# Second attention in quarters: the softmax weights of a query block are divided, turned and copied 32 queries at a time

## The chip, the cores and the metric

The kernel runs on one core of a Trainium2 chip. The metric is the device time of one execution in microseconds. A core has five engines with an instruction queue each: TensorE (PE: matmuls, and transposes as matmuls with an identity), VectorE (DVE), ScalarE (ACT), GpSimd (POOL) and SyncE (SP), which here only issues transfers. Each queue is worked off in order, and an instruction waits on semaphores for what others have to deliver. Matmul results land in PSUM, eight banks of 512 float32 columns on 128 partitions; everything else lies in the on-chip memory SBUF. Indirect transfers (gathers) are issued by GpSimd.

## The reference, cut to what matters

The reference is a network of two layers over `x` of 1 x 2048 x 128. Each layer is an attention and a mixture of experts, with residuals and layer norms. The change is in the second layer's attention, which chooses 96 keys per query: the 64 before it and 32 others by an index score.

```
x = x + attn0(norm(x)); x = x + experts0(norm(x))
x = x + attn1(norm(x)); x = x + experts1(norm(x))

def attn1(x):                                   # 8 heads
    c_kv = x @ W_dkv                            # 32 wide
    s_i = relu(einsum('bthd,bsd->bths', q_i, k_i))
    I = einsum('bths,h->bts', s_i, idx_w)       # index scores
    I = where(causal, -inf, where(local, inf, I))
    _, idx = top_k(I, 96)                       # 64 local, 32 chosen
    key_c, value = (c_kv @ W_uk)[idx], (c_kv @ W_uv)[idx]
    key_r = pope((x @ W_kr)[idx])               # rotated by rank
    scores = (q_c . key_c + q_r . key_r) * (64 + 32) ** -0.5
    attn = softmax(scores)                      # over the 96 keys
    return (attn @ value) @ W_out
```

The first attention has 16 heads of 64 over all 2048 keys (a full softmax); `experts0` takes 4 of 16 experts per token, `experts1` fixed ones of 8 and a shared one.

## The kernel before

**Tiling.** The 2048 tokens are 16 blocks n of 128, and four groups g of 512. The first attention works in 32 units, one for a pair of heads and a group (`UNITS`, line 280), in steps of 512 keys; a unit has four steps, and `run` (line 422) writes them out in order. In a step `by_query` (L323) makes scores by query, VectorE takes their maxima (L329), ScalarE sums exponentials (`sums`, L340); five steps behind, `by_key` (L384, L386) makes the scores again with keys on partitions, ScalarE takes exponentials into a tile `e` of 128 x 2 x 512 (L390), and `mean` (L399) multiplies them with the values, a pair of key blocks behind. The pool `a_e` (`self.ep`, line 274) has six such tiles, shared by `e` and by the temporaries `t_q`, `t_k` of `rope` (L302, L303).

**Beside it.** When a group of 512 queries has passed all eight units, its later stages (`follow`: `experts0`, `attention1`, `experts1`) run as a stream beside the next eight units: `advance` takes so much of the generator as its yields, which are costs in microseconds, allow. The last group's stream runs when the first attention is over (`self.alone`). So groups 0 to 2 are in the background and group 3 alone. The tile framework orders each engine's instructions by their place in the program and by when a cost model thinks them ready, and first attention's maxima and exponentials are raised in priority (`URGENT`); only SP's queue keeps the order in which it was written (`manual_schedule`). An instruction that needs a tile waits until a buffer of its tag is released.

**attention1 (line 725).** For a block of 128 queries: `index_scores` (L802 to L821) and `choose` (L835 to L842) search for the 32 keys of each query by repeated maxima on VectorE; the list is turned (L842), and 32 gathers on GpSimd (L853) bring the chosen rows `kv` of 128 x 32 x 64 from a table in device memory. In the background, gathers are issued by `pay`, one or more for every yield; alone, all at once. `queries` (line 866) loads the local rows `cl` by eight transfers of SP (L873) and makes the queries `ql`, `qs` (L877 to L908). `attend` (line 913) rotates the gathered rows (L97 to L104), turns them into `kr` (L932, L933), and makes the weights: in each quarter b, 32 queries with their 8 heads, two groups of 128 rows, TensorE adds a mask and the scores of 80 local and 128 gathered columns (L942, L950, L956) in a bank `pl`; VectorE takes the maxima (L962, L963); ScalarE writes exponentials and their sums (L966). After all four quarters the sums are inverted (L971), the weights divided (alone by ScalarE, eight instructions, L974; in the background by VectorE, one, L976), and turned on TensorE in four banks `pte` of four transposes (L983), each copied by ScalarE into `eT` (L984). Then the weighted sum of values `po` (L991, L998), its copy `lt` (L1005), the projection `pj` (L1012) and the addition to `xr` (L1013).

**Order in attention1.** Alone: search of 12, of 13, search of 14 with attend(12) beside it, of 15 with attend(13) beside it, then queries and attend of 14, and of 15. In PSUM the background has two banks (`x`, line 138), the stage alone cycles through all eight. `kr` and `eT` share one buffer (tag `w8`).

Of the kernel before, what the change touches and what calls it, by code (L numbers as in the profile page):

```python
# [17 lines left out]
P = 128  # L18
# [88 lines left out]
class Program:  # L107
# [161 lines left out]
    def pools(self):  # L269
        tc = self.tc  # L270

        self.first = ExitStack()
        self.qk = self.first.enter_context(tc.tile_pool(name="a_qk", bufs=3))
        self.ep = self.first.enter_context(tc.tile_pool(name="a_e", bufs=6))
        self.am = self.first.enter_context(tc.tile_pool(name="a_sm", bufs=2))
        self.negs, self.tops = {}, {}
        self.qs, self.ms, self.mrows, self.pos = {}, {}, {}, {}
        self.rs, self.outs, self.pts, self.kcs, self.csq = {}, {}, {}, {}, {}
# [446 lines left out]
    def attention1(self, sc, g):  # L725
# [60 lines left out]
        def pay(us):  # L786

            for _ in range(min(len(gathers), max(1, round(us / 1.8)))):
                gathers.pop(0)[1]()
            return us  # L790
# [75 lines left out]
        def queries(n):  # L866

            cl = sm.tile([80, 8, 32], F32, tag="cl", name=f"cl{n}", bufs=4 if self.alone else 2)  # L870
            for i in range(8):
                lo = max(n * P + 16 * i - 64, 0)
                nc.sync.dma_start(cl[:, i, :], table[lo : lo + 80, 0:32])  # L873
            chosen[n] = chosen[n], cl
            pq = self.x(f"pq{n}", [P, NH1, 64])
            q = slice(P * (n % 4), P * (n % 4) + P)
            nc.tensor.matmul(  # L877
                pq.rearrange("p a b -> p (a b)"), cqT[:, q], self.wq1.rearrange("p a b -> p (a b)"),
                start=True, stop=True,
            )  # L880
            qq = [
                sm.tile([P, 1024], F32, tag="w4", name=f"qq{n}_{i}").rearrange("p (h b d) -> p h b d", h=NH1, b=2)
                for i in range(2)
            ]
            mu = sm.tile([P, NH1, 32], F32, tag="mu", name=f"mu{n}", bufs=1)
            for i in range(2):
                nc.scalar.copy(qq[i][:, :, 0, 0:32], pq[:, :, 0:32])
            softplus(nc, sm, mu, pq[:, :, 32:64], self.one, "spq")
            yield pay(3.0)
            m4 = mu.rearrange("p h (a b) -> p h a b", a=2)  # L890
            for i, at in ((0, n), (1, NT + n)):
                q = qq[i][:, :, 0, :]
                rotate(
                    nc, nc.vector, sm, q[:, :, 32:48], q[:, :, 48:64], m4,
                    bcast(cs[:, 0, at, :], 1, NH1), bcast(cs[:, 1, at, :], 1, NH1), "rq", 1,
                )
                nc.scalar.copy(qq[i][:, :, 1, :], q)
                yield pay(1.5)
            qT = []
            for i in range(2):  # L900
                t = sm.tile([P, P, NH1], F32, tag=f"qT{i}", name=f"qT{n}_{i}", bufs=3 if self.alone else 1)
                for h in range(2):
                    pt = self.x(f"ptq{n}_{i}_{h}")
                    for j in range(4):
                        nc.tensor.transpose(
                            pt[:, j, :], qq[i][:, 4 * h + j, :, :].rearrange("p a b -> p (a b)"), ident
                        )
                    nc.scalar.copy(t[:, :, 4 * h : 4 * h + 4], pt.rearrange("p h q -> p q h"))  # L908
                    yield pay(1.0)
                qT.append(t.rearrange("p q h -> p (q h)"))  # L910
            qTs[n] = qT

        def attend(n):
# [14 lines left out]
            for q in range(4):  # L928
# [3 lines left out]
                    nc.tensor.transpose(pt[:, j, :], kv[:, s : s + 2, :].rearrange("p a b -> p (a b)"), ident)  # L932
                nc.scalar.copy(kr[:, 4 * q : 4 * q + 4, :], pt)  # L933
                yield pay(0.8)
            e = sm.tile([P, 8, NK], F32, tag="e1", name=f"e1_{n}", bufs=1)
            mx = sm.tile([P, 8], F32, tag="mx", name=f"mx1_{n}")
            su = sm.tile([P, 8], F32, tag="su", name=f"su1_{n}")
            ri = sm.tile([P, 8], F32, tag="ri", name=f"ri1_{n}")
            for b in range(4):
                rows = slice(64 * (b // 2), 64 * (b // 2) + 64)  # L940
                pl = self.x(f"pl{n}_{b}", [P, 2, NK])
                nc.tensor.matmul(  # L942
                    pl.rearrange("p a b -> p (a b)"), self.identb,
                    self.smask[:, 1 if n == 0 and b < 2 else 0].rearrange("p a b -> p (a b)"),
                    start=True, stop=False,
                )
                for c in range(2):
                    i = 2 * b + c
                    lo = max(n * P + 16 * i - 64, 0)
                    nc.tensor.matmul(  # L950
                        pl[:, c, 0:80], ql[rows, i * P : i * P + P], kT[rows, lo : lo + 80], start=False, stop=False
                    )
                for c in range(2):
                    for j in range(4):
                        gr = 4 * (2 * b + c) + j
                        nc.tensor.matmul(  # L956
                            pl[32 * j : 32 * j + 32, c, 80:NK], qs[rows, 32 * gr : 32 * gr + 32],
                            kr[rows, gr % 16, :], start=False, stop=(c == 1),
                        )
                yield pay(1.0)  # L960
                m2 = mx[:, 2 * b : 2 * b + 2]
                nc.vector.tensor_reduce(m2, pl, axis=AX.X, op=ALU.max)  # L962
                nc.vector.tensor_scalar(m2, m2, -SCALE1, None, ALU.mult)  # L963
                for c in range(2):
                    i = 2 * b + c
                    nc.scalar.activation(  # L966
                        e[:, i, :], pl[:, c, :], AF.Exp, scale=SCALE1, bias=mx[:, i : i + 1],
                        accum_out=su[:, i : i + 1],
                    )
                yield pay(1.5)  # L970
            nc.vector.reciprocal(ri, su)  # L971
            if self.alone:
                for i in range(8):
                    nc.scalar.activation(e[:, i, :], e[:, i, :], AF.Copy, scale=ri[:, i : i + 1])  # L974
            else:
                nc.vector.tensor_tensor(e, e, bcast(ri, 2, NK), ALU.mult)  # L976
            yield pay(2.0)
            eT = sm.tile([P, 16, P], F32, tag="w8", name=f"eT{n}", bufs=1).rearrange("p (k i) q -> p k i q", k=2)
            for k, (lo, hi) in enumerate(((0, 80), (80, NK))):
                for h in range(2):  # L980
                    pt = self.x(f"pte{n}_{k}_{h}")
                    for j in range(4):
                        nc.tensor.transpose(pt[: hi - lo, j, :], e[:, 4 * h + j, lo:hi], ident)  # L983
                    nc.scalar.copy(eT[: hi - lo, k, 4 * h : 4 * h + 4, :], pt[: hi - lo])  # L984
                    yield pay(0.8)

            po = self.x(f"po1_{n}", [P, 2, P])
            for c in range(2):
# [257 lines left out]
```

## Time and profile before

| what | us |
|---|---|
| median of three runs (2803.74 to 2807.57) | 2804.27 |
| the profiled execution | 2803.35 |
| its span in the trace | 2801.6 |
| TensorE busy | 2538.6 |
| ScalarE busy | 1789.8 |
| VectorE busy | 1670.8 |
| GpSimd busy | 671.3 |

The trace is of one execution. A page gives each engine's busy time, then the span in 40 slices (a digit is the busy share in tenths, and PEclk the clock that was granted to TensorE, in tenths of full speed), and groups of instructions by line, `out<-in`, with the number, the busy time, the mean of one, and the idle time of the engine just before them with what ended it. The timeline lists instructions by start and duration in us; a bracket gives the idle time before one and what ended it. An engine's busy time is an average over stages with different limits: in the table of slices TensorE is at nine tenths for most of the span and lower in the last eighth, where group 3 is alone.

### The profile page before, as it was taken

What the parts mean: (1) busy time and instruction counts of PE and PEld (TensorE: products, weight loads), DVE (VectorE), ACT (ScalarE), POOL (GpSimd) and SP (SyncE); (2) the same over time, 40 slices, a digit from 0 to 9 for tenths busy, and PEclk for the clock granted to TensorE, in tenths of its full rate; (3) what the DMA queues carried; (4) which work ended last, traced back from release to release, by engine and by line L of the source; (5) the groups of instructions that cost most, each with busy time, mean ns of one, the idle gap of its engine ahead of it and who ended that gap; (6) DMA issues with size and microseconds to landing.
All of it is one profiled execution on the core that took longest, in us unless ns stands there. A gap on an engine that the chain in (4) does not pass through costs nothing. (4 is left out here: it accounts for less than half of the span.)

```text
span 2801.6 us, 39304 instructions
## 1 busy us (share of the span) xinstructions
PE 2538.6 (91%) x13452; PEld 1170.6 (42%) x13452; DVE 1670.8 (60%) x4650; ACT 1789.8 (64%) x4192; POOL 671.3 (24%) x964
## 2 busy tenths in 40 slices
PE   6999999999989999999989999999989999975566
PEld 3444444434434444434334444444433444442344
DVE  7655554565664454566685455466687654288863
ACT  3777778866666776766666677755665677533343
POOL 2111110000166610000166630000055460001771
PEclk9999999999999999999999999999999999986566
DMA  4322221111111111111121111111011120100111
GB/s 134 88 61 61 57 61 46 44 43 50 30 43 48 48 37 55 49 45 38 33 48 43 48 33 59 42 43 48 25 38 37 37 49 16 63 23 12 26 26 38
DMA packets 98103, 127.79 MB, mean 46 GB/s; under 512 B 31344, under 2 KB 49776, under 8 KB 97904
## 3 DMA queue, kind: packets, MB, share of 16 engines
q1 hardware_dynamic: 81520, 108.48, 13.8%
q0 software_dynamic: 16384, 16.81, 2.9%
q8 instruction: 106, 1.74, 0.3%
q14 instruction: 93, 0.76, 0.1%
HBM read 115.26 MB, written 9.96 MB: 45 GB/s over the span
## 5 line engine op out<-in xcount | busy, mean ns | idle before, releaser
L340 ACT ACTIVATE neg<-neg,mx 128x512 f32<-128x512 f32 x1024 | 729.8, 714 | 305.3 <-DVE neg L329 296.6
L329 DVE TENSOR_SCALAR_CACHE_REDUCE neg<-pa 128x512 f32<-128x512 f32 x1024 | 657.7, 686 | 428.1 <-PE pa L323 423.4
L390 ACT ACTIVATE e<-pb 128x512 f32<-128x512 f32 x1024 | 550.4, 595 | 293.0 <-PE pb L386 280.1
L384 PE MATMUL pb<-q,kb 64*128 64x512 f32 x2048 | 638.8, 628 | 8.5 <-DVE t_q L302 5.2
L323 PE MATMUL pa<-ka,q 64*128 64x512 f32 x2048 | 597.7, 621 | 21.9 <-ACT e L390 15.0
L853 POOL DMA_INDIRECT kv<-table,ixT x512 | 506.3, 989 | 425.3 <-DVE v L804 266.9
L399 PE MATMUL po<-e,ckv 128*64 128x512 f32 x2048 | 511.7, 612 | 0.0
L323 PEld LDWEIGHTS pa<-ka,q 64*128 64x128 f32 x2048 | 245.2, 190 | 227.0 <-issue 101.7
L303 POOL TENSOR_TENSOR q<-t_q 128x512 f32<-128x512 f32 x32 | 40.8, 1274 | 1206.3 <-DVE t_q L302 1106.7
L384 PEld LDWEIGHTS pb<-q,kb 64*128 64x128 f32 x2048 | 225.4, 190 | 210.8 <-issue 106.1
L386 PE MATMUL pb<-mrow,onesb 64*128 64x512 bf16 x1024 | 252.5, 383 | 6.8 <-ACT mrow L375 6.8
L399 PEld LDWEIGHTS po<-e,ckv 128*64 128x64 f32 x2048 | 126.9, 137 | 301.0 <-issue 283.6
L340 ACT ACTIVATION_READ_ACCUMULATOR neg<-neg,mx 128x1 f32 x1024 | 192.3, 188 | 0.0
L802 PE MATMUL pi<-kiT,qiT 64*128 64x512 f32 (+4 forms) x320 | 110.0, 610 | 26.1 <-DVE v L804 14.7
L386 PEld LDWEIGHTS <-onesb 64*128 64x128 bf16 x1024 | 69.2, 96 | 127.4 <-issue 119.6
L418 DVE SCALAR_TENSOR_TENSOR xr<-pp,rs,xr 128x128 f32<-128x128 f32 x256 | 72.2, 344 | 82.6 <-PE pp L415 69.4
L850 POOL COPY at<-kv 128x1 f32<-128x1 f32 x378 | 77.8, 211 | 174.3 <-DMA kv<-table,ixT 168.8
L721 DVE SCALAR_TENSOR_TENSOR hb<-thb,zb 128x512 f32<-128x512 f32 x64 | 44.3, 692 | 113.2 <-ACT zb L719 113.1
L808 DVE SCALAR_TENSOR_TENSOR v<-rl,iw_sb,v 128x512 f32<-128x512 f32 (+4 forms) x120 | 76.4, 642 | 51.1 <-ACT rl L807 46.7
L966 ACT ACTIVATE e<-pl,mx 128x208 f32<-128x208 f32 x128 | 54.3, 429 | 81.1 <-DVE mx L963 79.5
L303 POOL TENSOR_TENSOR kst<-t_k 128x512 f32<-128x512 f32 x32 | 41.0, 1283 | 264.0 <-DVE t_k L302 168.2
L962 DVE TENSOR_REDUCE mx<-pl 128x2 f32<-128x416 f32 x64 | 37.7, 590 | 100.3 <-PE pl L956 99.9
(276 smaller groups left out, 2859.0 us busy)
## 6 DMA issues: line engine op xcount, KB each, us to landing
ka<-kd SPq DMA_DIRECT2D x128, 256.0 KB, 3.6
kb<-kd SPq DMA_DIRECT2D x128, 256.0 KB, 3.7
wb<-in_wx SPq DMA_DIRECT2D x64, 192.0 KB, 2.4
kd<-kst SPq DMA_DIRECT2D x32, 256.0 KB, 2.3
kv<-table,ixT POOLq DMA_INDIRECT x512, 2.5
wd<-in_wx SPq DMA_DIRECT2D x40, 192.0 KB, 3.7
csk<-in_cs SPq DMA_DIRECT2D x4, 512.0 KB, 6.7
csq<-in_cs SPq DMA_DIRECT2D x4, 512.0 KB
```

What stands on the lines that cost most here:

```text
L303: nc.gpsimd.tensor_tensor(dst, t[:, 0, :], t[:, 1, :], ALU.add)
L323: nc.tensor.matmul(ps[h], q[rows, qt * P : qt * P + P], k[rows, :], start=True, stop=True)
L329: nc.vector.tensor_scalar(t, ps[h], -1.0, None, ALU.mult, ALU.min, accum_out=mx[at])
L340: nc.scalar.activation(t, t, AF.Exp, bias=mx[at], scale=-1.0, accum_out=su[at])
L384: nc.tensor.matmul(ps[h], k[rows, c], q[rows, :], start=True, stop=False)
L386: nc.tensor.matmul(ps[h], self.onesb[rows, :], mrow[rows, :], start=False, stop=True)
L390: nc.scalar.activation(e[:, h, :], ps[h], AF.Exp)
L399: nc.tensor.matmul(self.pos[u][cols, :], self.ckv[:, kb, :], e[:, h, :], start=(kb == 0), stop=(kb == NT - 1))
L802: nc.tensor.matmul(pi[:, : hi - lo], qiT[h // 2][rows, q], kiT[rows, lo:hi], start=True, stop=True)
L808: nc.vector.scalar_tensor_tensor(v[:, lo:hi], rl[:, : hi - lo], w["iw"][:, h : h + 1], v[:, lo:hi], ALU.mult, ALU.add)
L850: tc.keep_in_program_order(nc.gpsimd.tensor_copy(at[:, i : i + 1], slot))
L853: nc.gpsimd.indirect_dma_start(out=kv[:, 2 * (g % 16) + g // 16, :], out_offset=None, in_=table[0 : P * (n + 1), :], in_offset=bass.Indire ...
```

## The change

The loop over quarters in `attend` runs five times. In turn b it makes the scores and exponentials of quarter b as before (b below 4) and then, for quarter b - 1, inverts its sums, divides its weights, turns them and copies them. The weights `e` lie in two buffers of one quarter each instead of one of the whole block. A bank `pte` now holds one quarter: both column ranges (80 and 128) of its two groups, copied by two instructions instead of one. `eT` has a buffer of its own. To make room, `cl` has one buffer instead of two in the background, and `a_e` has five tiles instead of six.

```diff
-        self.ep = self.first.enter_context(tc.tile_pool(name="a_e", bufs=6))
+        self.ep = self.first.enter_context(tc.tile_pool(name="a_e", bufs=5))
...
-            cl = sm.tile([80, 8, 32], F32, tag="cl", name=f"cl{n}", bufs=4 if self.alone else 2)
+            cl = sm.tile([80, 8, 32], F32, tag="cl", name=f"cl{n}", bufs=4 if self.alone else 1)
...
-            e = sm.tile([P, 8, NK], F32, tag="e1", name=f"e1_{n}", bufs=1)
+            es = {}
...
+            eT = sm.tile([P, 16, P], F32, tag="eT", name=f"eT{n}", bufs=1).rearrange("p (k i) q -> p k i q", k=2)
-            for b in range(4):
+            for b in range(5):
+                if b < 4:
+                    e = es[b] = sm.tile([P, 2, NK], F32, tag="e1", name=f"e1_{n}_{b}", bufs=2)
...
-                        e[:, i, :], pl[:, c, :], AF.Exp, scale=SCALE1, bias=mx[:, i : i + 1],
+                            e[:, c, :], pl[:, c, :], AF.Exp, scale=SCALE1, bias=mx[:, i : i + 1],
...
-            nc.vector.reciprocal(ri, su)
-            if self.alone:
-                for i in range(8):
-                    nc.scalar.activation(e[:, i, :], e[:, i, :], AF.Copy, scale=ri[:, i : i + 1])
-            else:
-                nc.vector.tensor_tensor(e, e, bcast(ri, 2, NK), ALU.mult)
-            yield pay(2.0)
-            eT = sm.tile([P, 16, P], F32, tag="w8", name=f"eT{n}", bufs=1).rearrange("p (k i) q -> p k i q", k=2)
-            for k, (lo, hi) in enumerate(((0, 80), (80, NK))):
-                for h in range(2):
-                    pt = self.x(f"pte{n}_{k}_{h}")
-                    for j in range(4):
-                        nc.tensor.transpose(pt[: hi - lo, j, :], e[:, 4 * h + j, lo:hi], ident)
-                    nc.scalar.copy(eT[: hi - lo, k, 4 * h : 4 * h + 4, :], pt[: hi - lo])
-                    yield pay(0.8)
+                if b == 0:
+                    continue
+                two, e = slice(2 * b - 2, 2 * b), es.pop(b - 1)
+                nc.vector.reciprocal(ri[:, two], su[:, two])
+                if self.alone:
+                    for c in range(2):
+                        i = 2 * b - 2 + c
+                        nc.scalar.activation(e[:, c, :], e[:, c, :], AF.Copy, scale=ri[:, i : i + 1])
+                else:
+                    nc.vector.tensor_tensor(e, e, bcast(ri[:, two], 2, NK), ALU.mult)
+                yield pay(0.5)
+                pt = self.x(f"pte{n}_{b}")
+                for k, (lo, hi) in enumerate(((0, 80), (80, NK))):
+                    for c in range(2):
+                        nc.tensor.transpose(pt[: hi - lo, 2 * k + c, :], e[:, c, lo:hi], ident)
+                for k, m in ((0, 80), (1, P)):
+                    nc.scalar.copy(eT[:m, k, two, :], pt[:m, 2 * k : 2 * k + 2, :])
+                yield pay(0.8)
```

## The prediction

> **What bounds the kernel.** I read the page's table of engines and its 40 slices first, then the totals by stretch, and then the last 240 us instruction by instruction.
>
> ```profile
> PE 2538.6 (91%) x13452; PEld 1170.6 (42%) x13452; DVE 1670.8 (60%) x4650; ACT 1789.8 (64%) x4192; POOL 671.3 (24%) x964
> PE   6999999999989999999989999999989999975566
> PEclk9999999999999999999999999999999999986566
> ```
>
> Up to about 2450 us TensorE sets the pace: between 700 and 2450 us, where groups 0 to 2 of the second attention run beside the first attention, it is busy 1652.7 of 1750 us (94%), VectorE 1020.5, ScalarE 1170.1. What is added to VectorE or ScalarE there costs only what makes TensorE stand. The tail, where group 3 runs alone, is a chain. The timeline, each line with its start and duration, reads for query block 15:
>
> ```profile
> 2704.75 0.21 DVE L842 STREAM_TRANSPOSE ixT<-ix 128x32 uint32<-128x32 uint32 x1
> 2705.70 0.94 POOL L853 DMA_INDIRECT kv<-table,ixT  x1 [2.92 <-issue]
> 2745.76 0.69 DVE L97 TENSOR_TENSOR w<-kv,cs 128x512 f32<-128x512 f32 x1 [1.44 <-DMA kv<-table,ixT]
> 2758.97 0.20 DVE L971 RECIPROCAL ri<-su 128x8 f32<-128x8 f32 x1 [1.07 <-ACT e L966]
> 2759.21 2.98 ACT L974 ACTIVATE e<-e,ri 128x208 f32<-128x208 f32 x8 [0.27 <-DVE ri L971]
> 2759.73 3.64 PE L983 MATMUL pte<-ident,e 128*80 128x128 f32 x16 [2.69 <-ACT e L974]
> 2763.19 1.55 ACT L984 COPY eT<-pte 80x512 f32<-80x512 f32 x3 [0.53 <-PE pte L983]
> 2767.88 3.78 PE L1012 MATMUL pj<-wvo,lt 32*128 32x128 f32 x16 [1.59 <-ACT lt L1005]
> 2771.69 0.29 DVE L1013 TENSOR_TENSOR xr<-xr,pj 128x128 f32<-128x128 f32 x1 [12.52 <-PE pj L1012]
> ```
>
> VectorE finishes choosing the keys of block 15 at 2704.96. GpSimd then issues 32 gathers, 1.25 us apart (2705.7 to 2745.9). Only then can attend(15) run, 2745.76 to 2771.98, and the last experts take the rest. Blocks 12 to 14 of attend lie beside the searches and gathers; shortening them moves nothing. Choosing 15 sooner gains at most 2.92 us, the gap on GpSimd in which it waited for the list; choosing later costs its full length.
>
> **The operations changed.** Groups by line: busy us, mean ns of one, then the engine's idle time before them.
>
> ```profile
> L984 ACT COPY eT<-pte 80x512 f32<-80x512 f32 (+1 forms) x64 | 35.4, 579 | 3.8 <-PE pte L983 3.6
> L976 DVE TENSOR_TENSOR e<-e,ri 128x1664 f32<-128x1664 f32 x12 | 23.8, 1979 | 0.3
> L974 ACT ACTIVATE e<-e,ri 128x208 f32<-128x208 f32 x32 | 11.9, 455 | 2.9 <-DVE ri L971 2.9
> L971 DVE RECIPROCAL ri<-su 128x8 f32<-128x8 f32 x16 | 3.2, 197 | 7.5 <-ACT e L966 7.5
> ```
>
> Reciprocals: 16 become 64; 48 more by 0.197 = +9.5 us of VectorE, three quarters of it in the 12 background blocks. Background division: 12 of 1.979 become 48 of 128x416; multiplications of 128x256 took 0.42 and of 128x512 0.69, so 0.59 is my estimate, 28.3 against 23.8, +4.5 us. Divisions in the tail stay 32 of 0.455. Copies of turned weights: 64 of 0.579 become 128 of half the width; a PSUM copy of 128x256 (line 887) took 0.375, so 48.0 against 37.1, +11 us of ScalarE. Transposes and matmuls keep number and shape: TensorE +0. In the background these add 12 us to VectorE and 8 us to ScalarE, under cover of TensorE's 94%; uncovered they would cost the 20.
>
> **attend(15), worked through.** It is the only attend on the chain. Now the reductions start at 2751.98, 2753.45, 2754.90 and 2757.11, the last exponential ends at 2758.94, and the sum over values ends at 2766.28. With quarters the divisions and copies of quarters 0 to 2 could lie beside scores. But the weights get two buffers instead of one of full size, so quarter 2's exponentials wait until quarter 0 is divided and turned. Step by step: exponentials 0 end at 2753.7; the reciprocal comes behind reduction 1 on VectorE, at 2754.4; exponentials 1 end at 2755.2; division 0 (two of 0.37, as eight took 2.98) ends at 2755.9, but TensorE is inside the fourth score block until 2757.05, so the four transposes end near 2758.0 (0.91, a quarter of 3.64). Copies 0 take 0.6 and exponentials 2 end at 2759.4, not 2756.6; copies 1, exponentials 3 and division 2 end at 2761.6; transposes 2 and division 3 at 2762.5; transposes 3 at 2763.4, copies 3 at 2764.1. The last copy now starts about 2764.2 and ends 2764.74. Behind it one quarter of the products is left instead of half a weight block, so the sum over values ends near 2765.8: gain 0.5 us. From both sides: if the scores of quarter 3 are queued ahead less tightly, -2.5; if TensorE reaches the transposes only after later work, +2.
>
> A rule of the Trainium skill bears here. The granted clock in two windows (us; busy PE, PEld, DVE, ACT, POOL; then the clock, DMA share, GB/s):
>
> ```profile
> 2754.00:2756.00 2.00, 2.00 (x28) 1.39 (x27) 0.97 (x4) 1.15 (x5) 0.00 (x0) 0.81 0.00 0
> 2760.00:2762.00 2.00, 2.00 (x11) 1.79 (x10) 0.00 (x0) 2.00 (x7) 0.00 (x0) 0.50 0.00 0
> ```
>
> "TensorE: Matmul & The Clock Gate" (Part 1) says that the clock halves after an idle window and recovers after about as long a busy one, about 3.4 us each. Transposes spread between score blocks would close the 2.69 us gap ahead of them; the 16 matmuls of pj then take 2.05 us as at 2704.43, not 3.78, and with the transposes the chain is 3.4 us shorter. The trace lets the clock fall to 0.81 in a stretch in which TensorE was busy all 2.00 us, so the gap did not cause it. By the rule the sum below ends at 2805.7, by the row at 2809; I take the row and keep -3.4 as the other end.
>
> **Choosing block 15.** attend(12) and attend(13) share VectorE with the searches. Its waits between 2560 and 2705 (total, times, longest):
>
> ```profile
> DVE mx L962 <- PE pl L956: 10.3, 7, 2.4
> DVE w L97 <- DMA kv<-table,ixT: 5.4, 1, 5.4
> ```
>
> VectorE executes in order, so a reduction that waits for scores holds up the search behind it. The change puts four transposes, 0.97 us at the halved clock (3.87 for 16 at 2642.11), between scores: ahead of two reductions per block, four in all, at most 3.9. Search passes of 2.2 us can fill part; half, 2.0, is my value, 0 and 3.9 the ends. Six more reciprocals by about 0.15 of occupied time add 0.9. So +2.9, and GpSimd's gathers and everything behind them move by it.
>
> **The background.** There quarter 2 and 3 wait for transposes as above: 24 new waits on ScalarE. The nearest rows (waits, total, times, longest; 700 to 2450):
>
> ```profile
> ACT e L966 <- DVE mx L963: 56.6, 36, 3.7
> PE pa L323 <- ACT e L390: 15.0, 16, 3.6
> ```
>
> A wait like the first lasts 1.57 us, so 24 make 38 us; queued behind are the exponentials of the first attention, and TensorE waits for their banks. ScalarE's waits there come to some 470 us for neg, e of both attentions; TensorE stood 31 us for ScalarE (15.0, 9.4 on kr, 6.3 on rl): 6.5%. So +2.5; ends 0 and, if half reaches TensorE, 19. Better filling of its 97 idle us could give back 3.
>
> **Edits at nothing.** *Five buffers for first attention's weights*: a pair of key blocks holds two, the pair before two until its products, which stand ahead of the next pair's scores on TensorE; the rotation's temporary takes the fifth. Where both q and k are rotated, six are wanted; at 246.17 GpSimd freed the temporary by 247.44, before the second pair of exponentials began near 247.9. Cost 0; uncovered, one GpSimd addition of 1.27 us at 7 such places is 9, at all 31 unit starts 39. *One cl buffer*: SP's loads of block n+1 now wait for the products of block n. Issue against the end of those: 923.5 and 929, 983.6 and 992.5, 1515.8 and 1528.6, 1583.6 and 1595.3, 1644.9 and 1656.9, 2217.4 and 2222.2, 2260.9 and 2278.8, 2322.8 and 2334.5. SP stands 5 to 18 us, and queued behind are ka and kb, next issued at 944.6, 1004.2, 1535.8, 1603.0, 1668.0, 2240.9, 2284.1, 2343.3: all later, and a step (some 20 us) ahead of use. Cost 0, cover gone: the excess over that step. *eT apart from kr*: kr waits for no eT in the trace; 0. *Three more calls to pay per block*: each may issue one waiting gather earlier on POOL; 0, since block 1 to 11 never waited for gathers.
>
> **Sum.** +2.9 - 0.5 + 2.5 = +4.9 us. The profiled execution took 2803.35 (span 2801.6 and 1.75 around it), 0.9 below the median of 2804.27; 4.9 on the median is 2809.2, rounded 2809.
>
> **Rivals.**
> - *In-order stalls reach TensorE.* Half of the 38 us on ScalarE, beside 2.9 in the tail: 2826; a third: 2820. For it: 94% busy leaves no reserve, and at 811 to 820 a late gather on VectorE did stop TensorE 8.1 us. Against: only 6.5% came through so far. It decides above some 5% more than my share. Chance 0.26.
> - *The fifth buffer binds* (slower): 7 to 31 starts by 1.27, 2815 to 2845. Against: the times at 246. Chance 0.10.
> - *The tail gains* (other side): clock kept (-3.4), GpSimd's gap closed (-2.9), no background cost: 2798. Against: the full-busy window at 0.81. It needs VectorE's order to lose 2.9 of its 10.3 waits. Chance 0.14.
> - *No overlap, no harm*: two buffers serialize the quarters, all else is hidden: 2804. Chance 0.08.
> - *Mine*: 0.42, its own range 2804 to 2814.
>
> 0.2% of 2804.27 is 5.6 us, about what a measurement tells from no change: below 2798.7 faster, above 2809.9 slower. Slower: 0.17 of mine, 0.25, 0.09: 0.51. Faster: 0.09 of the tail's gain and 0.01: 0.10. Same: 0.39. The range leaves out a tenth on each side: 2798 to 2827.
>
> **What would show it.** Right: 64 reciprocals, eT copies near 0.375; block 15's list later than 2704.96 by 1 to 5 us; in attend(15) exponentials of quarter 2 ending after the first transposes; ka issues unmoved after cl. Wrong: TensorE's waits for e of line 390 above 30 us (first rival), waits on GpSimd at unit starts (second), pj at 2.05 in block 15 and a list before 2703 (third).

## The result, and the profile after

The changed kernel takes 2818.78 us (median of five runs, 2817.14 to 2828.72), the kernel before 2804.27 (with two runs more than the three of the table above, 2802.11 to 2808.16): a ratio of 1.0054, 95% interval 1.0034 to 1.0074. It is slower by 14.5 us. A second set of runs, on a chip where the kernel before takes 2806.91, gave 2822.58, 1.0056 (1.0040 to 1.0072). The prediction said 2809.0, range 2798 to 2827.

The profiled execution was the slowest of its set both times: 2828.72 us, 9.9 above the median, and 2824.62, 2.0 above it. So I read both traces, and build on what they share. The engines in the first trace, with their busy time:

```profile
PE 2564.4 (91%) x13452; PEld 1181.2 (42%) x13452; DVE 1681.3 (59%) x4734; ACT 1792.5 (63%) x4256; POOL 668.6 (24%) x964
```

VectorE has 84 instructions more and ScalarE 64 more, and their busy time grew by 10.5 and 2.7 us. TensorE has the same number of instructions, and yet it is busy 25.8 us longer (21.8 in the second set): its granted clock, as a mean over the span, is 0.930 in both traces, where it was 0.942 (0.939 in the second set). The groups of the changed operations (busy us, mean ns of one, then idle time before them):

```profile
L991 ACT COPY eT<-pte 80x256 f32<-80x256 f32 (+1 forms) x128 | 41.4, 366 | 17.7 <-PE pte L989 17.5
...
L984 DVE TENSOR_TENSOR e<-e,ri 128x416 f32<-128x416 f32 x48 | 29.3, 611 | 1.5
...
L978 DVE RECIPROCAL ri<-su 128x2 f32<-128x2 f32 x64 | 10.3, 162 | 33.0 <-ACT e L970 32.7
```

These are the sizes that were worked out: 64 reciprocals, divisions of 0.61 (0.59 estimated), copies of 0.366 (0.375). The time is not lost in the operations themselves. The table shows the stretches in which it is lost; each row ends at one instruction of VectorE (us). The last column is the kernel before with its two buffer sizes changed, traced in the second set.

| stretch, up to | before | changed, 1st trace | changed, 2nd trace | before, with five tiles and one cl |
|---|---|---|---|---|
| start of group 3 | 2453.98 | 2465.72 | 2464.74 | 2457.22 |
| list of block 12 | 121.48 | 121.86 | 122.37 | 121.18 |
| list of 13 | 29.35 | 29.33 | 29.32 | 29.33 |
| list of 14 (attend of 12 beside it) | 46.80 | 42.25 | 41.74 | 46.76 |
| last index score of 15 | 15.91 | 26.25 | 24.89 | 15.79 |
| list of 15 (attend of 13 beside it) | 37.23 | 41.60 | 39.87 | 37.22 |
| addition of block 15 to xr | 66.94 | 69.99 | 69.20 | 66.97 |
| end of the span | 29.91 | 29.60 | 30.17 | 30.13 |
| span | 2801.6 | 2826.6 | 2822.3 | 2804.6 |

In the second set (the two last columns) the 17.7 us are 7.5 in the background, 1.2 up to list 12, then -5.0, +9.1 and +2.7 in the searches, and 2.2 behind list 15. So there are four places of loss to explain (the background, the scores of 15, list 15, attend of 15), and one stretch, the search of 14, is shorter.

**The search of 14 gains.** VectorE's waits between the start of the search and list 15, first trace (total, times, longest):

```profile
DVE xr L1020 <- PE pj L1019: 8.3, 2, 6.0
...
DVE mx L966 <- PE pl L960: 5.2, 5, 2.4
```

It waits 5.2 us for score blocks where it waited 10.3. TensorE now has one score block (quarter 2) between the transposes of quarter 0 and of quarter 1, so its reduction comes later, and search passes fill the time instead. List 14 comes 4.5 to 5.0 us earlier.

**The scores of 15 come late.** TensorE at the end of attend of 12, in the kernel before:

```profile
2642.11 3.87 PE L983 MATMUL pte<-ident,e 128*80 128x128 f32 x16 [5.58 <-ACT e L974]
...
2646.28 1.12 PE L802 MATMUL pi<-kiT,qiT 64*128 64x512 f32 x2
```

And in the first trace of the changed kernel:

```profile
2648.43 1.22 PE L989 MATMUL pte<-ident,e 128*80 128x128 f32 x4 [4.41 <-ACT e L982]
...
2652.01 1.07 PE L989 MATMUL pte<-ident,e 128*80 128x128 f32 x4
2657.54 2.08 PE L989 MATMUL pte<-ident,e 128*80 128x128 f32 x8 [4.46 <-ACT e L982]
...
2660.64 2.07 PE L802 MATMUL pi<-kiT,qiT 64*128 64x512 f32 x2
...
2666.07 3.78 PE L1019 MATMUL pj<-wvo,lt 32*128 32x128 f32 x16
```

In the kernel before it stood once for the divisions, 5.58 us ahead of all 16 transposes. Now it stands twice, 4.41 and 4.46 us. The divisions wait for reciprocals, and these stand on VectorE behind search passes of 2.1 us. The index scores of block 15 (L802) are queued behind: they start 1.5 us after list 14; in the kernel before it was 5.3 us ahead of it. VectorE, same trace:

```profile
2659.16 0.21 DVE L842 STREAM_TRANSPOSE ixT<-ix 128x32 uint32<-128x32 uint32 x1
2662.75 0.75 DVE L804 TENSOR_SCALAR v<-pi,iw_sb 128x512 f32<-128x512 f32 x1 [3.38 <-PE pi L802]
2666.80 0.75 DVE L808 SCALAR_TENSOR_TENSOR v<-rl,iw_sb,v 128x512 f32<-128x512 f32 x1 [3.30 <-ACT rl L807]
...
2685.41 0.29 DVE L821 TENSOR_TENSOR v<-v,vmask_sb 128x128 f32<-128x128 f32 x1
...
2718.58 2.22 DVE L837 FIND_INDEX8 ix<-m,v 128x8 uint32<-128x1984 f32 x1
2726.80 0.29 DVE L1020 TENSOR_TENSOR xr<-xr,pj 128x128 f32<-128x128 f32 x1 [6.01 <-PE pj L1019]
2727.01 0.20 DVE L842 STREAM_TRANSPOSE ixT<-ix 128x32 uint32<-128x32 uint32 x1
```

It now waits for the scores, 3.38 us at first, then for ScalarE's `rl`, which comes behind the copy `lt` of block 12; it has the last score 26.25 us after the list, not 15.91. About half of that difference is only that list 14 comes earlier: counted from list 13, the last score is 5.8 us later than in the kernel before (4.1 in the second set). Of these, 2.3 us (1.8) pass before the first of the scores, and 3.5 (2.3) between the first and the last. In that last stretch TensorE's granted clock differs as well. A window near its start, kernel before and first trace (us; busy PE, PEld, DVE, ACT, POOL; the clock, DMA share, GB/s):

```profile
2648.00:2652.00 4.00, 3.23 (x59) 2.36 (x51) 3.56 (x5) 2.32 (x6) 3.09 (x4) 1.00 0.16 29
...
2660.00:2664.00 4.00, 4.00 (x79) 2.05 (x76) 0.75 (x1) 0.29 (x2) 3.08 (x4) 0.50 0.15 32
```

From the first score to the last, the clock is at half for 13.6 us in the first trace and 8.4 in the second, and for 3.4 in the kernel before and in the one with changed buffers. How much of the delay is the order of the instructions and how much the clock, no run separates.

And at the end the search of 15 is done at 2720.8, but the addition of block 13's projection is ahead of the turning of the list, and VectorE stands 6.01 us for it. GpSimd's gathers, and all that follows, wait for the list. In the kernel before this addition came after the list of 2704.75:

```profile
2706.51 0.29 DVE L1013 TENSOR_TENSOR xr<-xr,pj 128x128 f32<-128x128 f32 x1 [1.55 <-PE pj L1012]
```

In the second trace of the changed kernel the order is the new one too, and VectorE stands 4.3 us.

**attend of 15.** TensorE, then VectorE, first trace:

```profile
2774.80 0.64 PE L960 MATMUL pl<-kr,qT 64*32 64x128 f32 x16
2777.75 0.43 PE L989 MATMUL pte<-ident,e 128*80 128x128 f32 x1 [2.31 <-ACT e L982]
...
2780.54 1.08 PE L960 MATMUL pl<-kr,qT 64*32 64x128 f32 x16
2781.55 1.07 PE L989 MATMUL pte<-ident,e 128*80 128x128 f32 x4
...
2783.97 1.08 PE L960 MATMUL pl<-kr,qT 64*32 64x128 f32 x16
```

```profile
2775.51 0.59 DVE L966 TENSOR_REDUCE mx<-pl 128x2 f32<-128x416 f32 x1 [0.68 <-PE pl L960]
...
2781.68 0.59 DVE L966 TENSOR_REDUCE mx<-pl 128x2 f32<-128x416 f32 x1 [4.14 <-PE pl L960]
...
2785.11 0.59 DVE L966 TENSOR_REDUCE mx<-pl 128x2 f32<-128x416 f32 x1 [2.63 <-PE pl L960]
```

The transposes of quarter 0 stand ahead of the third score block, so TensorE waits 2.31 us for the division and makes the scores of quarter 2 only then. The third and fourth reductions start 6.2 and 9.6 us after the second; in the kernel before 1.45 and 3.66. From the end of the last rotation (2772.50) to the copy `lt` (2791.64) it takes 19.1 us, in the second trace 19.5, before 16.5 (16.5 with changed buffers too).

**The background.** TensorE's waits that the prediction had named, between 700 and 2450 us, and one that it had not:

```profile
ACT e L970 <- DVE mx L967: 55.5, 35, 3.9
...
PE pa L323 <- ACT e L390: 17.6, 15, 5.2
...
PE pb L384 <- DVE t_q L302: 8.0, 4, 2.8
```

The wait for `e` of line 390 is 17.6 us in this trace and 13.7 in the second, against 15.0; it hardly moved. That for `t_q`, the start of a unit's rotation, rose from 5.2 to 8.0 (7.7 in the second trace, 3.7 in the kernel with only its buffers changed). But TensorE's idle time as a whole did not grow. The window from 700 to 2450 us, kernel with changed buffers and second trace:

```profile
700.00:2450.00 1750.00, 1651.03 (x9022) 743.05 (x9022) 1021.14 (x2916) 1170.02 (x2757) 478.80 (x781) 0.97 0.15 42
...
700.00:2450.00 1750.00, 1656.75 (x8982) 744.57 (x8982) 1032.41 (x2984) 1168.08 (x2794) 474.85 (x781) 0.96 0.15 42
```

TensorE is idle for 99.0 us of the window with the old loop and for 93.3 with the new one (97.3 and 97.6 in the first set), and does fewer instructions in it. What grew is the time at half clock, by the clock records of the traces: 85 and 89 us of this window with the old loop, 123 and 130 with the new.

One place has both. The last rotation of a unit, second trace, VectorE and TensorE, and then the windows with the granted clock:

```profile
2209.94 0.17 DVE L978 RECIPROCAL ri<-su 128x2 f32<-128x2 f32 x1 [0.66 <-ACT e L970]
2210.14 0.59 DVE L984 TENSOR_TENSOR e<-e,ri 128x416 f32<-128x416 f32 x1
2210.65 1.28 DVE L302 TENSOR_TENSOR t_q<-ps_q,csq 128x512 f32<-128x512 f32 x2
```

```profile
2208.04 0.59 PE L384 MATMUL pb<-q,kb 64*128 64x512 f32 x1
2211.39 1.22 PE L384 MATMUL pb<-q,kb 64*128 64x512 f32 x1 [2.76 <-DVE t_q L302]
```

```profile
2208.00:2212.00 4.00, 1.24 (x5) 0.50 (x3) 3.00 (x12) 2.48 (x9) 0.00 (x0) 0.83 0.00 0
2212.00:2216.00 4.00, 4.00 (x10) 2.31 (x9) 1.07 (x3) 1.90 (x4) 3.52 (x5) 0.50 0.05 8
2216.00:2220.00 4.00, 4.00 (x12) 1.19 (x11) 1.64 (x6) 2.86 (x8) 2.23 (x5) 0.50 0.07 16
```

A reciprocal waits 0.66 us for the sums of its quarter, then comes the division, and only then the rotation for which TensorE stands 2.76 us; for the next 8 us it runs at half clock. In the kernel with only its buffers changed, the rotation came ahead of both (VectorE, same place):

```profile
2207.34 1.29 DVE L302 TENSOR_TENSOR t_q<-ps_q,csq 128x512 f32<-128x512 f32 x2 [0.29 <-PE ps_q L299]
2208.54 0.19 DVE L971 RECIPROCAL ri<-su 128x8 f32<-128x8 f32 x1
```

There TensorE stands 2.06 us some 7 us ahead of the rotation, for ScalarE, and is at half clock for 3.4 us after it. Of the 7.5 us that the second trace loses up to group 3, 3.3 had been lost by this unit's rotation (2212.01 against 2208.71 on GpSimd), the rest after it. All four traces of kernels with quarters in the background, on chips like the result's, agree in this last part: TensorE stands 2.76 to 2.81 us here, half clock follows for 6.8 to 10.2 us, and from the start of the rotation on VectorE to that of group 3 it takes 254.1 to 259.1 us, against 249.4 and 249.9 with the old loop. Up to this rotation the four traces differ from that of the old loop in their set by -5.9 to +5.7 us, in both directions. So 4 to 10 us of loss in the last unit are common to all; for the rest of the background, and for the share of the clock, the cause is not shown.

### The profile page after: what moved, and what is told of

Read it like the earlier page. It is cut to its first block, busy times and chain, and to the rows that moved or that the text cites. A ratio compares the mean times of both kernels' runs of the same rounds, so it can differ in the third digit from the quotient of the medians.

```text
span 2826.6 us, 39530 instructions
## 1 busy us (share of the span) xinstructions
PE 2564.4 (91%) x13452; PEld 1181.2 (42%) x13452; DVE 1681.3 (59%) x4734; ACT 1792.5 (63%) x4256; POOL 668.6 (24%) x964
## 5 line engine op out<-in xcount | busy, mean ns | idle before, releaser
L323 PE MATMUL pa<-ka,q 64*128 64x512 f32 x2048 | 608.8, 631 | 22.6 <-ACT e L390 17.6
L802 PE MATMUL pi<-kiT,qiT 64*128 64x512 f32 (+4 forms) x320 | 113.1, 618 | 26.2 <-DVE v L804 15.9
```

Of the source, the lines that this page charges most:

```text
L323: nc.tensor.matmul(ps[h], q[rows, qt * P : qt * P + P], k[rows, :], start=True, stop=True)
L802: nc.tensor.matmul(pi[:, : hi - lo], qiT[h // 2][rows, q], kiT[rows, lo:hi], start=True, stop=True)
```

## The experiments

The first two sets of four ran on chips where the kernel before takes 2920 us, not 2804; the third set ran on one like that of the result. What this means for the reading is said with each.

**Which blocks cost.** Four kernels, each with the loop by quarters in some blocks and the old code in the others. With quarters in the background the buffers are those of the change, else those of before. The kernel before was timed on these chips but left no trace there.

```diff
+            if n < 12:
...
+            else:
...
```

The other three have `n >= 12`, `n == 15` and `n in (12, 13)`.

> The quarters, the five tiles and the single cl buffer in blocks 0 to 11, blocks 12 to 15 as in the kernel before. Theory 1, the tail: the two traces differ by 12.9 us behind the start of block 12's search (10.2 up to the list of block 15, 2.7 in attend of 15), so of 14.5 us only 1.6 are left for the background: 2806, between 2803 and 2809. Rival, the background: the trace of the changed kernel reaches group 3 11.7 us later, because ScalarE and VectorE stall TensorE: 2816.

> The quarters in blocks 12 to 15 alone, the background as in the kernel before, with six tiles and two cl buffers. Theory 1: +12.9, 2817, and the list of block 15 is ready 10 us later counted from that of block 12. Rival, the background: +3, 2807.

> The quarters in block 15 alone. Theory 1: the search is untouched, and attend of block 15 is 2.7 us longer because TensorE has the transposes of quarter 0 ahead of the third block of scores and stands for the division: 2807. The prediction's own step had 0.5 shorter: 2803.8.

> The quarters in blocks 12 and 13 alone, whose attend lies beside the searches of 14 and 15. Theory 1: +10.2, 2814.5, with VectorE standing some 6 us for the projection of block 13 ahead of the turning of list 15. The prediction's step (reductions held up, reciprocals): +2.9, 2807. If attend of 12 and 13 is hidden beside the searches: 2804.

Measured against the kernel before on that chip: quarters in the background 0.9959 (0.9938 to 0.9979); in blocks 12 to 15 1.0144 (1.0109 to 1.0180); in block 15 1.0013 (0.9994 to 1.0032); in blocks 12 and 13 1.0135 (1.0099 to 1.0171). So blocks 12 and 13, whose attend lies off the chain, cost nearly all of the tail's loss, as theory 1 has it. Their 39 us are four times its 10, though, so the size is no size of the result's chip. The trace of quarters in blocks 12 to 15, all engines, shows what is added (here L1066 is the copy `lt`):

```profile
2720.01 0.94 POOL L853 DMA_INDIRECT kv<-table,ixT  x1 [23.93 <-DVE ixT L842]
...
2758.71 0.94 POOL L853 DMA_INDIRECT kv<-table,ixT  x1 [0.30 <-issue]
2765.23 1.49 ACT L1066 COPY lt<-po 32x256 f32<-32x256 f32 x4 [44.57 <-remote]
...
2767.37 0.75 DVE L808 SCALAR_TENSOR_TENSOR v<-rl,iw_sb,v 128x512 f32<-128x512 f32 x1 [43.50 <-ACT rl L807]
```

List 14 starts 32 gathers at 2720.01; ScalarE stands 44.57 us, until 5.6 us after the last is issued, and VectorE with it. In the same place of the kernel with quarters in blocks 12 and 13 it is 44.58 us. With the tail of the kernel before (quarters in the background) ScalarE stood 12.0 us while the gathers of 14 streamed: attend of 12 was done when they began. But that tail has long stands as well, in the search of 14 while the gathers of 13 stream:

```profile
2695.60 1.10 DVE L1023 TENSOR_REDUCE mx<-pl 128x2 f32<-128x416 f32 x2 [37.73 <-remote]
```

This search takes 78 to 85 us in all eight traces on these chips, with quarters in the tail or without, and 42 to 47 on the result's. So the stands are not the change's own; it has list 14 earlier and attend of 12 later, and so puts one more piece of the chain under the gathers. In the traces of the result's chip no such stand is seen. That the gathers cause it is argued from their times, not shown.

Block 15 alone: from the last rotation to `lt` 19.5 us (2863.38 to 2882.90), as in the changed kernel; no such stand falls into this stretch. The ratio's interval holds the expected 2.7 us, and zero too.

**The background again.**

> The same kernel as the one with the quarters in blocks 0 to 11 alone, with another set of runs. In the first set it took 0.9959 of the kernel before. Theory 1, the tail alone costs: between 0.996 and 1.001 again. Rival, the background costs what the trace of the changed kernel showed (+11.7 us at the start of group 3): 1.004.

0.9976 (0.9950 to 1.0002). On these two chips quarters in the background, with the change's buffers, gain or cost nothing: the four traces with them reach group 3 at 2466.5 to 2480.5, the four without at 2480.4 to 2511.5. On the result's kind of chip it is the other way: with them 2465.72, 2464.74, 2465.17 and 2460.53 in four traces, without them 2453.98 and 2457.22, so 3 to 12 us later. These are single traces, and the two sides touch; the reason for the opposite sign is not settled.

**List 15 ahead of the addition.** A data dependence that adds nothing to the result: for block 13 alone, the addition takes a factor of one made from the list of 15, and stands in the program behind the searches.

```diff
             nc.vector.transpose(ixT, ix)
+            if n == 15:
+                s = sm.tile([P, 1], F32, tag="after15", name="after15", bufs=1)
+                nc.vector.tensor_scalar(s, ixT[:, 0:1], 0.0, 1.0, ALU.mult, ALU.add)
+                late.append(s)
...
-            nc.vector.tensor_tensor(xr[:, n % 4, :], xr[:, n % 4, :], pj, ALU.add)
+            def add(s=self.one):
+                nc.vector.scalar_tensor_tensor(xr[:, n % 4, :], pj, s[:, 0:1], xr[:, n % 4, :], ALU.mult, ALU.add)
+
+            if n == 13:
+                late.append(add)
+            else:
+                nc.vector.tensor_tensor(xr[:, n % 4, :], xr[:, n % 4, :], pj, ALU.add)
...
```

> The changed kernel with one dependency more: the addition of block 13's projection to xr takes a factor of one that is made from the list of block 15, so VectorE turns the list first; nothing else moves on any engine. Theory 1: in the trace of the changed kernel the list came 6.2 us after its last search pass, because VectorE stood 6.01 us for that projection; now the list follows its search at once, and the time is 6 us below the changed kernel's (2812.8 where the kernel before takes 2804.3, +0.3% instead of +0.54%). Rival: the gathers are not what sets the end, the wait moves on: same as the changed kernel, +0.54%.

VectorE at the end of that search:

```profile
2797.53 2.22 DVE L837 FIND_INDEX8 ix<-m,v 128x8 uint32<-128x1984 f32 x1
2799.78 0.21 DVE L842 STREAM_TRANSPOSE ixT<-ix 128x32 uint32<-128x32 uint32 x1
...
2804.05 0.35 DVE L1025 SCALAR_TENSOR_TENSOR xr<-pj,after,xr 128x128 f32<-128x128 f32 x1 [3.88 <-PE pj L1023]
```

The list follows its last pass at once, and the wait for the projection, 3.88 us here, stands behind it. From the last score to the list it takes 35.42 us; the three kernels with the addition ahead took 39.86, 41.60 and 41.61 on these chips. So this one place in VectorE's order makes the list 4.4 to 6.2 us later. That the end of the kernel moves by as much is not shown: in this trace list 15 to the addition of block 15 takes 104.2 us, in the other traces of these chips 91.6 to 100.9, and the time, 1.0094 (1.0061 to 1.0127), can't be set against the changed kernel's, which did not run on that chip.

**The scores of 15 ahead.** Matmuls, ScalarE's `rl` and VectorE's sums of block 15's index scores raised in priority.

```diff
+                    with tc.high_priority(URGENT) if n == 15 else ExitStack():
                         nc.tensor.matmul(pi[:, : hi - lo], qiT[h // 2][rows, q], kiT[rows, lo:hi], start=True, stop=True)
```

> The changed kernel with the index scores of block 15 (TensorE, ScalarE, VectorE) raised in priority, so that they stand ahead of the weighted sum and the projection of block 12 on TensorE and ScalarE. Theory 1: in the trace of the changed kernel the scores of block 15 were complete 26.3 us after list 14, against 15.9 before; now some 5 us of that 10 come back: +0.35% over the kernel before instead of +0.54%. Rival: the delay is VectorE's own work (more reciprocals, more passes between), and the scores' place changes nothing: +0.54%.

1.0121 (1.0085 to 1.0156). This tells nothing of the 5 us: ScalarE stood 41.79 us ahead of `lt` all the same, with the other `rl` behind it, and from list 14 to the last score it took 75.9 us, against 66.6 in the kernels without it.

**All scores of block 15 first.** Quarters in block 15, four buffers for the weights, and two loops in place of one: scores and exponentials, then divisions.

```diff
-            for b in range(5):
+            for b in range(8):
                 if b < 4:
-                    e = es[b] = sm.tile([P, 2, NK], F32, tag="e1q", name=f"e1_{n}_{b}", bufs=2)
+                    e = es[b] = sm.tile([P, 2, NK], F32, tag="e1q", name=f"e1_{n}_{b}", bufs=4)
...
-                if b == 0:
+                if b < 4:
                     continue
+                b -= 3
```

> The quarters in block 15 alone, with four buffers for the weights, and the program has all four blocks of scores and exponentials ahead of the first division. Theory 1: TensorE no longer stands between score blocks; from the last rotation of the gathered rows to the end of the weighted sum it takes about 16.1 us (16.4 in the kernel before, 19.1 in the changed one), as ScalarE still has 8 divisions and 8 copies to do: the time is that of the kernel before, within 1 us. Rival: the halved clock and the split copies cost it anyway: 19 us, +0.1%.

TensorE, the last score block and the first transposes:

```profile
2864.45 0.64 PE L961 MATMUL pl<-kr,qT 64*32 64x128 f32 x16
2865.02 0.31 PE L991 MATMUL pte<-ident,e 128*80 128x128 f32 x1
```

The scores run on without a stand (the reductions start 1.45 us apart, at 2862.26, 2863.71 and 2865.16), and from the last rotation to `lt` it takes 15.9 us (2858.77 to 2874.71): 3.6 less than with the change's order. The old loop took 14.9, 15.0 and 15.5 us for this in the traces of these two chips that have it in block 15, so all scores first is still 0.4 to 1.0 us longer than the old loop. (The 16.5 of the kernel before are from another chip, and from an execution with more of this stretch at half clock.) So most of the loss in attend of 15 is TensorE's order together with the two buffers, and not the narrower copies or divisions. The two causes were lifted in one edit; what each does alone was not tried. The time is 1.0014 (0.9997 to 1.0031): the half microsecond is not to be seen.

**The changed kernel again, and its gathers held.** The third set, on a chip where the kernel before takes 2806.91 us. In the second kernel the gathers of 14 read a copy of the list that is made from the last score of 15. GpSimd issues in order, so the gathers of 15 still come behind them.

```diff
+            if n == 15:
+                z = sm.tile([P, 1], F32, tag="z15", name="z15", bufs=1)
+                nc.vector.tensor_scalar(z, v[:, width - 1 : width], 0.0, None, ALU.mult)
+                held = sm.tile([P, RK], U32, tag="held", name="held14", bufs=1)
+                nc.vector.tensor_scalar(held, ixTs[14], z[:, 0:1], None, ALU.add)
```

> The changed kernel itself, where the runs of the parts were made (the kernel before takes 2920 us there). If the parts add up: quarters alone 1.0144, background 0.996 and 0.998, so 1.011; and the changed kernel with list 15 ahead, 1.0094, has 6 us less than it, so 1.0115. Between list 14 and list 15 some 107 us, as in the kernel with quarters in blocks 12 and 13 alone (108.2). Rival, the ratio is that of the first runs, 1.0054: then the parts disturb each other.

> The changed kernel; only the start of block 14's 32 gathers is moved, behind the last index score of block 15 (they read the list through a copy that is made from it). Theory 2, engines stand while gathers stream, and the chain stands with them if its next work is what is caught: in the traces of these runs ScalarE stood 44.6 us ahead of block 12's copy of the weighted sum, from the start of those gathers to their end. Held, list 14 to the last score of 15 falls from 66.6 to about 27 us, and the stand moves with the gathers into the search of 15 (41.6 to some 65): about 15 us less than the changed kernel. Rival, it is the order of the instructions on TensorE and ScalarE or the clock alone: 66 us as before, and the time that of the changed kernel.

The changed kernel gave 1.0056, its rival's number: the parts' ratios hold on the chips where they were measured, not here. With the gathers held it took 2829.28 us, 1.0081 (1.0063 to 1.0100): not 15 us less than the changed kernel, and not the same, but 6.7 us more in the medians, with intervals that overlap. List 14, the last score of 15 and the first held gather:

```profile
2658.34 0.21 DVE L850 STREAM_TRANSPOSE ixT<-ix 128x32 uint32<-128x32 uint32 x1
...
2684.56 0.29 DVE L821 TENSOR_TENSOR v<-v,vmask_sb 128x128 f32<-128x128 f32 x1
...
2687.59 1.14 POOL L862 DMA_INDIRECT kv<-table,held  x1 [16.01 <-DVE held L827]
```

It takes 26.22 us from list to score with the gathers of 14 held, against 24.89 and 26.25 without. The test is weaker than it looks: the gathers of 13 are still being issued, up to 2670.64 here and up to 2671.84 and 2672.42 in the changed kernel, and those of 14 came only behind them, in the last 10 to 12 us of the stretch. But in the kernel with changed buffers gathers are issued all through the same stretch, and it takes 15.79 us. So on this kind of chip the gathers of 14 have no part in the delay, and gathers as such don't bring it; what is left is the rival, the order on TensorE and ScalarE and the clock. On the other kind the test was not made.

The same edit to the kernel with the quarters in blocks 0 to 11:

> The quarters in blocks 0 to 11, blocks 12 to 15 as in the kernel before, and block 14's gathers held as in the run beside it. Theory 2: in the kernel before those gathers catch some 12 us (64 us from list 14 to 15, against 53 in the first runs), and held they catch the search of 15 instead: no gain, 0.997 to 1.003 of the kernel before. If the held gathers catch less: 0.993, the fastest of all.

1.0047 (1.0028 to 1.0066), not the gain or the zero expected. The search takes what it took before (37.43 us from last score to list 15), but block 15's gathers now queue behind those of 14 on GpSimd: the last is issued 47 us after list 15, not 40, and the addition of block 15 comes 76.45 us after it, not 66.97. That is 9.5 of the 13.4 us that this trace is longer than that of the kernel with changed buffers; 3.3 lie before group 3.

**The buffers alone.**

> The kernel before with five tiles for the first attention's weights and one cl buffer in the background, nothing else. The prediction's step: 0, so 1.000 within 0.002. Its rival (the fifth buffer binds): 7 to 31 places of 1.27 us, 1.003 to 1.014.

```diff
-        self.ep = self.first.enter_context(tc.tile_pool(name="a_e", bufs=6))
+        self.ep = self.first.enter_context(tc.tile_pool(name="a_e", bufs=5))
...
-            cl = sm.tile([80, 8, 32], F32, tag="cl", name=f"cl{n}", bufs=4 if self.alone else 2)
+            cl = sm.tile([80, 8, 32], F32, tag="cl", name=f"cl{n}", bufs=4 if self.alone else 1)
```

1.0007 (0.9994 to 1.0020). No version was found that beats the kernel before on the result's kind of chip.

## Why the prediction was right, and where not

The direction was right and the time lies in the range, but it is 9.8 us above the forecast and outside the likeliest case's own 2804 to 2814: 14.5 us lost where 4.9 were expected. That the range holds it is in part luck, as its upper end came from rivals whose mechanisms are not what the traces show. The sum had +2.9, -0.5 and +2.5; measured, in the first trace against before and in the second against the kernel with changed buffers, are +10.1 and +6.7 (list 12 to list 15), +3.1 and +2.2 (list 15 to the addition), and 3 to 12 in the background, from all six traces.

**Right.** The operations' sizes. The edits at nothing: 1.0007 for tiles and cl. In the second trace of the changed kernel one of SP's loads of cl is at 930.15 us, where it was at 923.49, and the next ka still comes 19.9 us after the one before it (22.0 in the kernel before). Exponentials of quarter 2 in attend of 15 end after the first transposes. That a later list moves all behind it by its full length.

**Choosing block 15: a failed step.** "A reduction that waits for scores holds up the search behind it", put at +2.0, has the wrong sign: waits for scores fell by 5 us and list 14 came 4.5 to 5.0 earlier. What costs is on the other side of the handshake. A quarter now needs two visits to VectorE, each behind a pass of 2.1 to 2.2 us, and TensorE stands for the answer with block 15's index scores behind it. From list 13 to the last of these scores, the early list 14 included, that is +5.8 and +4.1 us, part of it perhaps the clock's. I had followed who waits on VectorE, and not what is queued behind the transposes on TensorE. And "GpSimd's gathers and everything behind them move by it" was right, but that an addition of block 13 could come to stand ahead of the list was not looked for: +4.4 and +2.7 us between the last score and list 15 (a wait of 6.0 and 4.3, less what the passes gained).

**attend of 15: a failed step.** "TensorE is inside the fourth score block until 2757.05, so the four transposes end near 2758.0": the scores are not queued ahead. The program has the transposes of quarter 0 ahead of the third score block, and TensorE keeps to it. The gain of 0.5 is not found with the order that the step assumed and four buffers either: 15.9 us, where the old loop took 14.9 to 15.5 on the same chips. So the term has the wrong sign in both orders.

**The background.** The step looked for ScalarE's waits that come through to TensorE. By the prediction's own sign the first rival is out: TensorE's waits for `e` of line 390 are 17.6 and 13.7 us, not above 30. What does reach TensorE comes by VectorE, where a reciprocal and a division now can stand ahead of a unit's rotation (+2.8 and +4.0 us of waits); but other waits fell, and TensorE's idle time stayed where it was. The time at half clock, some 40 us more of it, was in no term. The second rival's 2815 to 2845 holds the measured time, but the fifth buffer does not bind: 1.0007 with the buffers alone. And more than half of the loss is not in the background at all.

**The clock.** The Trainium skill, "TensorE: Matmul & The Clock Gate" (Part 1), gives some 3.4 us of busy time for the clock to recover. The windows above, from 2212 to 2220 us, show 0.50 over two of 4 us, busy all of both: here the row stands again. Neither of the two ends that I weighed came: the gap ahead of the transposes, 2.69 us, was not closed but split (2.31, 0.72 and 0.75 in the first trace), and pj of block 15 took 3.78 us in the first trace and 2.56 in the second. "TensorE +0" holds for the number and shape of the matmuls; their busy time grew by 25.8 and 21.8 us.

## What to carry to other kernels

To cut a chain of steps into quarters multiplies the handshakes between engines (in the tail, five visits to VectorE per block become eight), and each answer then waits behind whatever its engine has in hand, here a pass of 2 us; count, for each new wait, what is queued behind the one who waits. Work that is off the chain is not free if it shares an in-order engine with the chain: ask what stands behind it, and whether a result that is needed at once can come to lie behind an addition that nobody needs. Pipelining over quarters wants all first halves ahead of the first second half in the program, and buffers for them; here even that only took most of the loss back. And before an experiment is read against a number of another chip, look for the same stretch, with the old code, in a trace of its own.

## What the runs showed of the hardware

On two chips engines stood while GpSimd's gathers streamed: ScalarE 44.6, 44.6, 44.6 and 41.8 us in the four kernels with quarters in blocks 12 and 13, each time until 5.0 to 5.6 us after the issue of the last gather of the row had ended. TensorE meanwhile issued one to five matmuls every 0.7 to 2.1 us for some 10 us, and then stood as well. The old loop has stands of this kind there too (VectorE 37.7 us). On the result's kind of chip the same instructions show none. What they stood for, the trace does not say. The Trainium skill, "Runtime: NRT & Kernel Launch" (Instruction fetch mechanics), says that engines stream their code by DMA and that this is mostly hidden; if it is code that they stood for, it was not hidden here, but no run tests it.

In one block the clock can weigh as much as the change did. In the trace of the kernel with quarters in blocks 0 to 11 and the gathers of 14 held, block 15 has the old loop and TensorE is at half clock throughout: the reductions start 2.54 us apart, and from the last rotation to `lt` it takes 19.5 us. The same instructions, in the kernel without the hold on another chip, with half clock for 3.4 us of this stretch, took 1.45 us and 14.9.
